# Second passes of a three-layer cross attention by blocks of four chunks, and a low-rank sum moved to a later layer

## The chip, the core and the metric

The kernel runs on one core of a Trainium2 chip. The metric is the device time of one execution in microseconds (us). A core has engines that run side by side, each with its own in-order queue: PE (TensorE: matrix products, the results in PSUM; PEld is its loading of the stationary operand), DVE (VectorE), ACT (ScalarE), POOL (GpSimd) and SP (SyncE, which here issues most of the transfers). An f32 matmul of the code leaves two records in the trace.

## The reference

A model of four layers works on x, 128 rows of 256. Every layer is a cross attention over a context of 12544 rows of 192, then a self attention over the 128 rows, then a mixture of eight experts (FFN); each is added to x after a layer norm. The change lies in the cross attentions of layers 0, 1 and 2, each of 16 heads of 16, and in two weights of layer 3's. In short, with scale 1/4:

```python
q, k, v = heads(x @ Wq + bq), heads(ctx @ Wk + bk), heads(ctx @ Wv + bv)
attn = einsum('bhqd,bhkd->bhqk', q, k) * scale   # 128 x 12544 scores for each of 16 heads
attn = clip(attn, -10000., 10000.)               # layer 1 only; layer 0 has a mask of keys
x = einsum('bhqk,bhkd->bqhd', softmax(attn), v) @ Wo + bo
```

In layer 3 the heads are 64 wide, and the key and value weights have a low-rank part: `k_in = ctx @ Wk + ctx @ k_down @ k_up * alpha / 32`, and the same for v.

## The kernel before

**Keys and groups.** The context's 12544 keys are 98 chunks of 128; four chunks make a block of `SB` = 512 keys (`NSB` = 25 blocks, the last of two chunks). The heads are worked on in two groups g of eight. Each head of 16 takes one of four row groups of 32 rows in the stationary operand, so `tiles` are four slices of 32 partitions and a "half" is two of them; s is which of two heads in a row group.

**PSUM in these layers.** `attend_twice` (L501) gives all of PSUM to four tiles from `self.pair()`, each 128 x 2 x 512 f32. While the second pass runs, one of them is `acc`, the weighted sums; so three rotate among the score groups. A new tile is the oldest one, and the instruction that first writes it waits until that one's last reader is through.

**First pass** (L607 to L614): for each block, `highest` makes the scores of two row groups (L538; in layer 0 with a mask added by a bf16 matmul, L537) and DVE takes their maximum over the keys (L539). Keys and values are projected between (`keys.project`, L102). The mask's rows come from `mask_rows` (L519): a transfer on SP's queue (L524), and two POOL operations (L526, L527), for each block.

**Between the passes** `lowered` (L541) turns minus the maximum into three bf16 parts, laid in `wide` and transposed (L556). `m` (L558) holds them as rows, copied twice side by side. In layer 1, `floor` (L633) is the lower limit of the clip.

**Second pass** (L638): a step of two chunks calls `weights` for half 0 and half 1 and then `weighted` for the step before (in layer 1 two steps before). `weights` takes a pair tile, adds minus the maximum with two bf16 matmuls of 512 (L567), and adds the products of keys and queries with four f32 matmuls of 256 (L575). The exponential goes to an SBUF tile `e` (4 of them, 6 in layer 1): in layer 0 by two ACT operations of 512, with the mask as a bias column for each chunk (L581); in layer 1 by a clip on DVE (helper L289, called at L586) and ACT in place (L587); in layer 2 by one ACT operation of 1024 (L583). `weighted` (L590) multiplies v, 17 columns with a one for the sum, by e: 16 f32 matmuls of 128 for two chunks (L595), added up in `acc`. After 49 steps DVE copies `acc` to `oT` (L649). The order on each engine is that of a scheduling framework; `in_order` (L224) makes the instructions of chosen engines stay as they were written.

**The low-rank part** of layer 3. `prepare_l3` (L959) runs in layer 0's cross attention as `between`: after block 3 of the first pass it loads alpha, the down and up factors and the two weights of 1 MB, and at the end of each group's first pass PE multiplies down by up (`mm`, L275, four f32 matmuls of 512 with 32 rows in each group) ahead of the transpose L556, and DVE adds the product times `rate` to the weight (L289). `keys_l3` (L1054) then projects early keys of layer 3 during layer 2's self attention and FFN: eight `early_pair` products (L102, tile `kv`, one pair of banks in turn), whose context comes by POOL's queue.

**FFN weights.** `large_weights` (L1676) has ten tiles of 1 MB in layers 0 and 2, four in the others. They are loaded by SP's queue as tiles come free.

Of the kernel before, what the change touches and what calls it, by code (L numbers as in the profile page):

```python
# [205 lines left out]
class Net:  # L206
    def __init__(self, tc, d, ctx):
# [9 lines left out]
        self.broad = pool("broad", 1)  # L217
        self.banks = ExitStack()
# [179 lines left out]
    def load_mask(self, pool):  # L398
# [20 lines left out]
        self.ts(mf, mf, 1.0, -NEG, ALU.subtract, ALU.mult)  # L419
        self.ts(mf, mf, self.any[:nr], None, ALU.mult)  # L420
        t = self.tr()
        nc.tensor.transpose(t[:, 0, :nr], mf, self.ident[:nr, :nr])
        self.mask_col = self.cp.tile([P, nr], F32, tag="maskcol", name="maskcol")
        nc.vector.tensor_copy(self.mask_col, t[:, 0, :nr])
# [82 lines left out]
    def attend_twice_in(self, pool, o, qz, keys, masked, clip, between):  # L507
# [5 lines left out]
        if masked:  # L513

            rows8 = [pool.tile([P, SB], U8, tag=f"mask{i}", name="mask", bufs=1) for i in range(3)]
            for r in rows8:
                nc.gpsimd.memset(r, 1)

        def mask_rows(g, b):  # L519

            src = d["mask"].rearrange("c p -> (c p)")[b * SB : min(S2, b * SB + SB)].unsqueeze(0)
            n = src.shape[-1]
            to = rows8[b % 3]
            nc.sync.dma_start(to[0:P:32, :n], src.to_broadcast([4, n]))  # L524
            row = pool.tile([P, SB], BF16, tag="row", name="row", bufs=3)
            nc.gpsimd.tensor_scalar(row[:, :n], to[:, :n], 0.0, 1.0, ALU.is_gt, ALU.subtract)  # L526
            nc.gpsimd.tensor_scalar(row[:, :n], row[:, :n], self.bar, None, ALU.mult)  # L527
            return row
# [32 lines left out]
        def weights(g, c, half, m, floor):  # L561


            x = self.pair()
            for i in range(2):
                r = tiles[2 * half + i]
                nc.tensor.matmul(x[:, i, :], self.ones16[r, :], m[r, :], start=True, stop=False, skip_group_check=True)  # L567
            kT = keys.kT(c // 4)
            for j in range(2):
                k = slice((c % 4 + j) * P, (c % 4 + j + 1) * P)  # L570
                for i in range(2):
# [3 lines left out]
                    nc.tensor.matmul(at, kT[r, k], q, start=False, stop=True, skip_group_check=True)  # L575
            e = pool.tile([P, 2, 2, 2, P], F32, tag="e", name="e", bufs=4 if clip is None else 6)
            to = e.rearrange("p i j s q -> p i (j s q)")
            if masked:
                for j in range(2):
                    part = slice(j * HB, (j + 1) * HB)  # L580
                    nc.scalar.activation(to[:, :, part], x[:, :, part], AF.Exp, bias=self.mask_col[:, c + j : c + j + 1])  # L581
            elif floor is None:
                nc.scalar.activation(to, x, AF.Exp)  # L583
            else:

                self.stt(to, x, 0.0, floor[half], ALU.min, ALU.max)  # L586
                nc.scalar.activation(to, to, AF.Exp)  # L587
            return e

        def weighted(g, c, es, acc):  # L590
            v = keys.v(c // 4)
            for j in range(2):
                for s in range(2):
                    for t in range(4):
                        nc.tensor.matmul(  # L595
                            acc[32 * t : 32 * t + 17, s, :P], v[:, c % 4 + j, 2 * t + s, :], es[t // 2][:, t % 2, j, s, :],
                            start=c + j == 0, stop=c + j == S2 // P - 1,
                        )

        for g in range(2):  # L600
# [6 lines left out]
            for b in range(NSB):  # L607
                if masked:
                    rows.append(mask_rows(g, b))
# [16 lines left out]
            if clip is not None:  # L626
                floor = []
                for half in range(2):
# [5 lines left out]
                    self.ts(floor[half], x, -clip, None, ALU.add)  # L634
            acc = self.pair()
            nc.vector.memset(acc[:, :, :P], 0.0)
            made = []
            for c in range(0, S2 // P, 2):  # L638
                made.append((g, c, [weights(g, c, half, m, floor) for half in range(2)], acc))
                if len(made) > (1 if clip is None else 2):  # L640
                    weighted(*made.pop(0))
# [4 lines left out]
            for step in made:  # L646
                weighted(*step)
# [213 lines left out]
    def l0_xattn(self, x):  # L861
        nc, d = self.nc, self.d
        with self.tc.tile_pool(name="x0", bufs=2, reuse_waits="tile") as pool:
# [15 lines left out]
            with self.tc.tile_pool(name="layer3", bufs=1, reuse_waits="tile") as other:  # L879
                self.attend_twice(o, qz, keys, masked=True, between=self.prepare_l3(other))  # L880
# [78 lines left out]
    def prepare_l3(self, pool):  # L959


        nc, d, own = self.nc, self.d, self.broad
        dims = H * 64
        self.rate = own.tile([P, 4], F32, tag="rate", name="rate")
        self.w3 = []
        parts = []

        def add_low(i, k, down, up, w):
            made = []

            def products(bank_pair):
                for c in range(2):
                    p = bank_pair()
                    for h in range(2):
                        self.mm(p[:, h, :], [(down[:, c * P : (c + 1) * P], up[:, h * 512 : (h + 1) * 512])])
                    made.append(p)

            def sums():
                for c, p in enumerate(made):
                    part = w[:, c, :].rearrange("p (h e) -> p h e", h=2)  # L980
                    self.stt(part, p, self.rate[:, i : i + 1], part, ALU.mult, ALU.add)

            return products, sums

        def load():
# [755 lines left out]
```

## Time and profile before

| what | us |
|---|---|
| median of three runs | 3110.43 (3102.11 to 3118.96) |
| profiled execution, its own time | 3103.82 |
| its span | 3102.1 |
| second passes of layer 0, both groups: windows 162.1 to 297, 438.9 to 568.6 | 134.9, 129.7 |
| of layer 1: 822 to 950.7, 1090.9 to 1214.9 | 128.7, 124.0 |
| of layer 2: 1502.7 to 1630, 1774 to 1894.7 | 127.3, 120.7 |
| layer 0's FFN weights, DMA share between 640 and 689 | 0.84 |
| layer 2's self attention, 1896 to 1950, DMA share | 0.94 |

The windows of the first groups hold some projections of the second group too, and those of layer 0 the low-rank products. The granted clock of PE was 0.973 of full speed over the span.

How the profile is read: a row of a group gives line, engine, operation, tiles written and read, shapes and how many, then busy us, mean ns of one, and the idle time of the engine before them with what ended it. A timeline row gives start, duration from first start to last end, engine, line, operation, tiles, and how many were put together; in brackets, how long the engine had been idle and what ended that. Many instructions of PE overlap, so starts tell more than ends.

### The profile page before, as it was taken

The page shows a single profiled execution, that of the slowest core. Times are in us where ns is not written, and L with a number is a line of the kernel's source. Part 1 is how long each engine was busy: PE and PEld are TensorE (multiplying, and loading weights), DVE is VectorE, ACT ScalarE, POOL GpSimd, SP SyncE. Part 2 cuts the span into 40 slices and gives each one's busy share as a digit, 9 for nine tenths or more (in the row PEclk, how much of TensorE's full clock was granted, in tenths as well). Part 3 has the DMA queues.
Part 4 walks back from the last instruction along what each step waited for, and adds up shares of the span by engine and source line. Part 5 has one row for each costly group of instructions (what it writes and reads, how often), then busy time and mean ns, then how long its engine had stood idle before and what let it go on. Part 6 is the DMA issues. An engine that isn't in the chain of part 4 may idle for free.

```text
span 3102.1 us, 78224 instructions
## 1 busy us (share of the span) xinstructions
PE 2958.3 (95%) x35065; PEld 2247.1 (72%) x35065; DVE 1954.4 (63%) x2300; ACT 1470.4 (47%) x1869; POOL 296.2 (10%) x349
## 2 busy tenths in 40 slices
PE   9999999879999999899999999899999999999979
PEld 6677667645576576665676576489889889889858
DVE  6811860439997897769208703467777777777854
ACT  1188139511383176311572275256556556556521
POOL 6600640112000000110000001000000000000000
PEclk9999999999999999999999999899999999999979
DMA  4100210552002102441102105332223232223436
GB/s 131 56 18 21 69 47 3 186 206 58 27 3 62 50 18 73 126 133 50 31 8 72 50 3 194 129 86 82 86 78 88 81 86 81 85 79 88 123 112 204
DMA packets 165254, 246.83 MB, mean 80 GB/s; under 512 B 19853, under 2 KB 106831, under 8 KB 164920
## 3 DMA queue, kind: packets, MB, share of 16 engines
q1 hardware_dynamic: 160200, 227.67, 24.1%
q0 software_dynamic: 4608, 14.16, 1.4%
q8 instruction: 275, 4.51, 0.6%
q14 instruction: 59, 0.48, 0.1%
q10 hardware_dynamic: 112, 0.01, 0.0%
HBM read 241.65 MB, written 0.13 MB: 78 GB/s over the span
## 4 chain that ended last, share of the span: by engine, by line
PE 80%; DVE 11%; ACT 5%; issue 2%; DMA 1%; POOL 1%; SPq 0%; DVEq 0%; ACTq 0%; POOLq 0%
PE pair L102 20%; PE pair L538 10%; PE pair L575 9%; PE pair L595 8%; PE v L102 7%; PE sc L701 6%; PE acc L743 5%; PE ps L275 4%; DVE parts L539 4%; ACT e L581 3%; PE pair L567 3%; PE kv L102 2%; PE acc L275 2%; PE ps L1532 1%; PE pair L537 1%
## 5 line engine op out<-in xcount | busy, mean ns | idle before, releaser
L539 DVE TENSOR_REDUCE parts<-pair 128x2 f32<-128x1024 f32 x600 | 679.1, 1197 | 103.7 <-PE pair L538 103.6
L102 PE MATMUL pair<-ctxA,wk 128*128 128x256 f32 x1236 | 328.9, 399 | 1.4 <-ACT kT L193 1.1
L649 DVE COPY oT<-pair 128x256 f32<-128x256 f32 x6 | 2.5, 424 | 508.4 <-PE pair L595 508.4
L102 PEld LDWEIGHTS pair<-ctxA,wk 128*128 128x128 f32 x1236 | 217.0, 190 | 140.0 <-DVE parts L539 96.0
L538 PE MATMUL pair<-kT,qz 32*128 32x512 f32 (+1 forms) x1632 | 277.7, 615 | 9.8 <-DVE parts L539 9.6
L703 ACT COPY kept<-sc 128x1024 f32<-128x1024 f32 (+1 forms) x135 | 136.3, 1009 | 261.3 <-PE sc L701 261.3
L286 DVE TENSOR_TENSOR top<-top,kept 128x1024 f32<-128x1024 f32 (+2 forms) x145 | 169.1, 1169 | 133.9 <-ACT kept L703 132.6
L575 PE MATMUL pair<-qz,kT 32*128 32x256 f32 x3168 | 251.6, 374 | 0.0
L581 ACT ACTIVATE e<-pair,maskcol 128x512 f32<-128x512 f32 x392 | 237.1, 688 | 18.7 <-PE pair L575 17.5
L289 DVE SCALAR_TENSOR_TENSOR e<-pair,floor 128x1024 f32<-128x1024 f32 x196 | 230.4, 1219 | 7.5 <-PE pair L575 1.7
L587 ACT ACTIVATE e<-e 128x1024 f32<-128x1024 f32 x196 | 207.2, 1057 | 38.5 <-DVE e L289 30.9
L583 ACT ACTIVATE e<-pair 128x1024 f32<-128x1024 f32 x196 | 189.9, 1021 | 60.2 <-PE pair L575 60.2
L595 PE MATMUL pair<-e,v 128*17 128x128 f32 x6336 | 212.3, 274 | 2.0 <-ACT e L587 1.0
L575 PEld LDWEIGHTS pair<-qz,kT 32*128 32x128 f32 x3168 | 205.3, 187 | 10.8
L132 ACT ACTIVATE kT<-pair,bk 128x512 f32<-128x512 f32 (+1 forms) x68 | 45.9, 674 | 346.8 <-PE pair L102 346.8
L595 PEld LDWEIGHTS pair<-e,v 128*17 128x17 f32 x6336 | 156.6, 97 | 67.1 <-issue 42.5
L701 PE MATMUL sc<-qz,kT 64*128 64x128 f32 x2816 | 197.8, 279 | 0.0
L567 PE MATMUL pair<-low,ones 32*128 32x512 bf16 x1176 | 191.7, 391 | 3.6 <-DVE low L558 3.1
L102 PEld LDWEIGHTS v<-wv,ctxA 128*128 128x128 f32 x1568 | 189.8, 192 | 6.4 <-issue 1.7
L102 PE MATMUL v<-wv,ctxA 128*128 128x128 f32 x1568 | 193.1, 276 | 0.0
L102 PE MATMUL pair<-ctxB,wk 64*128 64x256 f32 x1236 | 188.3, 398 | 0.0
L701 PEld LDWEIGHTS sc<-qz,kT 64*128 64x128 f32 x2816 | 171.6, 187 | 13.0 <-issue 1.3
(425 smaller groups left out, 4859.3 us busy)
## 6 DMA issues: line engine op xcount, KB each, us to landing
ctxA<-in_ctxA SPq DMA_DIRECT2D x324, 256.0 KB
ctxB<-in_ctxB SPq DMA_DIRECT2D x339, 128.0 KB
w<-in_L_ffn_W SPq DMA_DIRECT2D x32, 1024.0 KB
ctxA<-in_ctxA POOLq DMA_DIRECT2D x36, 256.0 KB, 3.6
w<-in_L_ffn_w_gateT SPq DMA_DIRECT2D x8, 1024.0 KB
wu<-in_L_ffn_w_upT SPq DMA_DIRECT2D x8, 1024.0 KB
w<-in_L_ffn_w_downT SPq DMA_DIRECT2D x8, 1024.0 KB
w<-in_L_ffn_w1T SPq DMA_DIRECT2D x8, 1024.0 KB
```

What stands on the lines that cost most here:

```text
L102: self.nc.tensor.matmul(out, a, b, start=start and not low, stop=low == 1, skip_group_check=True)
L275: self.nc.tensor.matmul(out, lhsT, rhs, start=(i == 0), stop=(i == n - 1))
L289: self.nc.vector.scalar_tensor_tensor(out, a, s, b, op0, op1, **kw)
L538: nc.tensor.matmul(x[:, i, :n], qz[r, g, s, :], keys.kT(b)[r, :n], start=not masked, stop=True)
L539: nc.vector.tensor_reduce(parts[:, s, 2 * half : 2 * half + 2, b], x[:, :, :n], AX.X, ALU.max)
L567: nc.tensor.matmul(x[:, i, :], self.ones16[r, :], m[r, :], start=True, stop=False, skip_group_check=True)
L575: nc.tensor.matmul(at, kT[r, k], q, start=False, stop=True, skip_group_check=True)
L581: nc.scalar.activation(to[:, :, part], x[:, :, part], AF.Exp, bias=self.mask_col[:, c + j : c + j + 1])
L583: nc.scalar.activation(to, x, AF.Exp)
L587: nc.scalar.activation(to, to, AF.Exp)
L595: nc.tensor.matmul(acc[32 * t : 32 * t + 17, s, :P], v[:, c % 4 + j, 2 * t + s, :], es[t // 2][:, t % 2, j, s, :], start=c + j == 0, stop= ...
L701: nc.tensor.matmul(x[:, t, c : c + P], kT[r, c : c + P], qz[r, g, :], start=True, stop=True)
```

## The change

1. The second pass goes by blocks of four chunks. `weights(g, b, ...)` makes four product groups (chunks 0 and 1 of half 0, then half 1, then chunks 2 and 3 of the same), then `weighted` of the block before is issued, 32 matmuls. There are eight e tiles (seven in layer 2), and DVE and ACT keep the written order.
2. Layer 0: the mask is added by the matmul that adds minus the maximum. Its stationary is a second set of mask rows made on POOL for each block of the second pass (a transfer, two POOL operations), with ones in rows 0 to 2 of each row group and the mask in row 3; it takes four matmuls of 256 for each group, with four loads of the stationary, instead of two of 512 with two. The exponential is then one ACT operation of 1024. The mask's column form and its transpose go.
3. Layer 2: minus the maximum of half 1 is spread once by PE and kept in `less`; DVE adds it to the scores while it copies them to e, and ACT takes the exponential in place, after both exponentials of half 0 of the block. Half 0 stays as it was.
4. The low-rank part leaves layer 0 and stands at the head of `keys_l3`: loads, DVE scaling of down by rate, on PE down times up plus the identity times the weight (16 f32 matmuls of 512), four ACT copies back. The weights lie in a pool of their own, the low-rank factors too, and the pool `narrow` is moved to the other side of the memory.
5. `large_weights` has 12 tiles in layer 0 and 9 in layer 2.

```diff
-        def mask_rows(g, b):
+        def mask_rows(b, second=False):
...
-            nc.gpsimd.tensor_scalar(row[:, :n], row[:, :n], self.bar, None, ALU.mult)
+            if second:
+                nc.gpsimd.tensor_scalar(row[:, :n], row[:, :n], self.bar, three, ALU.mult, ALU.add)
+            else:
+                nc.gpsimd.tensor_scalar(row[:, :n], row[:, :n], self.bar, None, ALU.mult)
...
+        def products(g, c, half, m, row):
+            x = self.pair()
+            kT = keys.kT(c // 4)
+            for i in range(2):
+                r = tiles[2 * half + i]
+                if row is not None:
+                    for j in range(2):
+                        at = slice(j * HB, (j + 1) * HB)
+                        k = slice((c % 4 + j) * P, (c % 4 + j + 1) * P)
+                        nc.tensor.matmul(x[:, i, at], row[r, k], m[r, at], start=j == 0, stop=False, skip_group_check=True)
+                elif m is not None:
+                    nc.tensor.matmul(x[:, i, :], self.ones16[r, :], m[r, :], start=True, stop=False, skip_group_check=True)
...
+        def weights(g, b, m, floor, less):
+            row = mask_rows(b, True) if masked else None
+            made, later = [], []
+            for c in range(4 * b, min(4 * b + 4, S2 // P), 2):
+                es = []
+                for half in range(2):
+                    by_dve = less is not None and half == 1
+                    x = products(g, c, half, None if by_dve else m, row)
+                    e = pool.tile([P, 2, 2, 2, P], F32, tag="e", name="e", bufs=7 if less is not None else 8)
...
+                    if by_dve:
+                        by_chunk = to.rearrange("p i (j n) -> p i j n", j=2)
+                        self.tt(by_chunk, x.rearrange("p i (j n) -> p i j n", j=2), bc(less, 2, 2), ALU.add)
+                        later.append(to)
+                    elif floor is not None:
+                        self.stt(to, x, 0.0, floor[half], ALU.min, ALU.max)
+                        nc.scalar.activation(to, to, AF.Exp)
+                    else:
+                        nc.scalar.activation(to, x, AF.Exp)
+                made.append((c, es))
+            for to in later:
+                nc.scalar.activation(to, to, AF.Exp)
+            return made
...
-            for c in range(0, S2 // P, 2):
-                made.append((g, c, [weights(g, c, half, m, floor) for half in range(2)], acc))
-                if len(made) > (1 if clip is None else 2):
-                    weighted(*made.pop(0))
+            last = []
+            with self.in_order(mybir.EngineType.DVE, mybir.EngineType.Activation):
+                for b in range(NSB):
+                    now = weights(g, b, m, floor, less)
+                    weighted(last, acc)
+                    last = now
...
+    def prepare_l3(self):
...
+        for i, k in ((1, "k"), (2, "v")):
+            w = self.load_kv(d[f"L3_xattn_W{k}"], dims, f"w{k}", self.wp3)
...
+            self.ts(down, down, self.rate[:RANK, i : i + 1], None, ALU.mult)
...
+            for c in range(2):
+                p = self.early_pair()
+                for h in range(2):
+                    cols = slice(h * 512, (h + 1) * 512)
+                    self.mm(p[:, h, :], [(down[:, c * P : (c + 1) * P], up[:, cols]), (self.ident, w[:, c, cols])])
+                nc.scalar.copy(w[:, c, :].rearrange("p (h e) -> p h e", h=2), p)
...
     def keys_l3(self):
+        self.prepare_l3()
...
-            with self.large_weights(bufs=10 if by_place else 4) as self.wp:
+            with self.large_weights(bufs={0: 12, 2: 9}.get(layer, 4)) as self.wp:
```

## The prediction, written before the result was known

> **What bounds the kernel now.** I read the page's engine lines, its chain of waits and its groups first, then the windows of the second passes one by one, then the timeline inside them.
>
> ```profile
> PE 2958.3 (95%) x35065; PEld 2247.1 (72%) x35065; DVE 1954.4 (63%) x2300; ACT 1470.4 (47%) x1869; POOL 296.2 (10%) x349
> ...
> PE 80%; DVE 11%; ACT 5%; issue 2%; DMA 1%; POOL 1%; SPq 0%; DVEq 0%; ACTq 0%; POOLq 0%
> ...
> L581 ACT ACTIVATE e<-pair,maskcol 128x512 f32<-128x512 f32 x392 | 237.1, 688 | 18.7 <-PE pair L575 17.5
> L289 DVE SCALAR_TENSOR_TENSOR e<-pair,floor 128x1024 f32<-128x1024 f32 x196 | 230.4, 1219 | 7.5 <-PE pair L575 1.7
> L587 ACT ACTIVATE e<-e 128x1024 f32<-128x1024 f32 x196 | 207.2, 1057 | 38.5 <-DVE e L289 30.9
> L583 ACT ACTIVATE e<-pair 128x1024 f32<-128x1024 f32 x196 | 189.9, 1021 | 60.2 <-PE pair L575 60.2
> ```
>
> TensorE is the bound (95% busy, 80% of the chain), so a PE that waits is lost time. The four groups read what a second pass writes to PSUM: ACT in layer 0 (L581), DVE then ACT in layer 1 (L289, L587), ACT in layer 2 (L583). The windows view (us; then busy PE, PEld, DVE, ACT, POOL; clock, DMA share, GB/s) gives one second pass of layers 0, 1 and 2:
>
> ```profile
> 162.10:297.00 134.90, 134.09 (x2607) 100.46 (x2606) 3.44 (x4) 122.27 (x202) 0.00 (x0) 0.96 0.05 15
> ...
> 1090.90:1214.90 124.00, 122.74 (x2552) 92.02 (x2546) 117.47 (x102) 103.61 (x98) 0.00 (x0) 1.00 0.03 7
> 1774.00:1894.70 120.70, 119.98 (x2548) 90.10 (x2548) 1.28 (x4) 96.06 (x99) 0.00 (x0) 1.00 0.01 3
> ```
>
> By the timeline, from the first L567 to the oT copy and without the 6.05 us of projections in each first group, the six passes last 124.0 and 124.8 (layer 0), 122 and 123.9 (layer 1), 121.4 and 120.5 us (layer 2): 49 steps of two chunks at 2.43 us. One steady step of layer 2:
>
> ```profile
> 1564.79 0.39 PE L567 MATMUL pair<-low,ones 32*128 32x512 bf16 x2
> 1565.01 0.38 PE L575 MATMUL pair<-qz,kT 32*128 32x256 f32 x2
> 1565.03 0.39 PE L567 MATMUL pair<-low,ones 32*128 32x512 bf16 x2
> 1565.23 1.05 PE L575 MATMUL pair<-qz,kT 32*128 32x256 f32 x14
> 1566.21 1.07 PE L595 MATMUL pair<-e,v 128*17 128x128 f32 x32
> 1567.21 0.39 PE L567 MATMUL pair<-low,ones 32*128 32x512 bf16 x2
> ```
>
> Two product groups (one per half; the halves use different rows of the array and overlap) take 1.42 us, the weighted sum 1.00. Two groups need two pairs of banks, three rotate (the fourth holds acc): a group finds its pair free.
>
> **Part 1: blocks of four chunks.** A block issues four groups, g1 to g4, and then the weighted sum of the block before (64 records instead of 32). With three rotating pairs, g4 takes the pair of g1 of its own block, and must wait until g1 has been computed and read. In the built order this holds in all three layers, and the weighted sum stands behind g4 on PE's in-order queue, so it can't fill the wait, and the next block's g1 and in the end the oT copy wait behind both. Before had this once: at the start of a pass no weighted sum stands between the first two steps. Layer 2, second group of heads:
>
> ```profile
> 1774.12 0.39 PE L567 MATMUL pair<-low,ones 32*128 32x512 bf16 x2 [0.79 <-DVE low L558]
> ...
> 1775.30 0.39 PE L567 MATMUL pair<-low,ones 32*128 32x512 bf16 x2
> ...
> 1775.48 3.77 ACT L583 ACTIVATE e<-pair 128x1024 f32<-128x1024 f32 x4 [6.11 <-PE pair L575]
> ...
> 1776.55 0.39 PE L567 MATMUL pair<-low,ones 32*128 32x512 bf16 x2
> ...
> 1777.73 1.07 PE L595 MATMUL pair<-e,kv 128*17 128x128 f32 x32
> ```
>
> g1 starts at 1774.12, its reader 1.36 later; spacing of readers is (3.77−1.02)/3 = 0.92; g4 starts at 1776.55, 2.43 after g1, though g1 and g2 needed 1.18 and g3 one half's work. From g4 to the weighted sum it is 1.18. So a block costs 1.36 + 1.07 (read, release) + 1.18 = 3.61, plus four chunks weighted at 1.89 (less one switch) to 2.00: **5.50 us where two steps took 4.85**.
>
> By layer. *Layer 0*: the mask enters by matmuls: per half 4 weight loads and 4 bf16 matmuls of 256 replace 2 and 2 of 512, the same columns; no row shows this form, so 0 (same columns) to +0.2 us per block (two extra 0.09 loads per half, half of them bare): 5.60. ACT does 4×0.92 = 3.7 instead of 8×0.61 = 4.88, hidden below PE now. POOL makes two rows per block (1.93 + 1.57 us by L526, L527), once more per pass, 25 mask DMAs more on SP's queue: 3.5 of 5.6 us, ahead of use, hidden; uncovered only if POOL were over 5.6. *Layer 1*: the reader is DVE at 1.22, so g4 starts at 1.36+1.22+0.05 = 2.63, block 5.70; DVE itself needs 4×1.13 = 4.52 (1.13 is the spacing in its unbroken runs), no longer the limit. *Layer 2*: half 1's subtraction goes from PE (L567) to DVE, g4 shortens from 1.18 to 0.96: 5.28 as lower bound. But DVE writes g4 into one of only seven e tiles, the one whose weighted sum of the block before is just running; ACT's exps are in order, so half 1's exps stand ahead of the next block's g1, and delay g4 there: weighted start +1.2 (tile free) +1.2 (DVE) + two exps of 1.13 puts the next g1's read 1.0 later: 5.6. I take 5.6, bounds 5.2 and 5.9.
>
> A pass has 24.5 blocks: the first without weighted sum 3.6, 23 at the period, 4.4 for the half block, its exps and two weighted sums. Layer 0: 3.6 + 23×5.6 + 4.4 = 136.8, plus 2 (10.2 us at half clock at the start of each pass): +14 each, **+28** (22 to 36). Layer 1: 3.8 + 23×5.7 + 4.9 + 1.5 (floors) = 141.3: **+36** (30 to 42). Layer 2: 136.8: **+31** (16 to 40).
>
> The Trainium skill, TensorEngine Tiling (Array Packing), section Key Properties, says that a change of tiling mode drains the array, which speaks for larger blocks, and its section PSUM Bottleneck warns that reading PSUM, not the array, may then bound and advises both ScalarE and VectorE as readers. The step above agrees with the first (1.42 for two groups before a switch, 1.18 in the run of four), by which alone the six passes would gain some 0.24×24.5×6 = 35 us; the second is what 1774 to 1777 shows, and by its advice layer 2 with two readers would be at its lower bound of 5.28, but g4 waits for one read, which a second reader doesn't shorten.
>
> **Part 2: layer 3's low-rank part.** It leaves layer 0's first passes, where its products stood on PE ahead of L556:
>
> ```profile
> 162.13 3.69 PE L275 MATMUL pair<-up,down 32*128 32x512 f32 x8
> 165.75 0.44 PE L556 MATMUL pair<-ident,wide 128*128 128x128 f32 x2
> ```
>
> That saves 2×3.65 = **−7.3**. It comes back ahead of the early keys of layer 3 in layer 2's attention and FFN: 12 DMAs on SP's queue, behind up to nine FFN weights of 1 MB (two weights of 1 MB in three DMAs each, two for each down, one for each up), 2 small DVE scalings, 16 f32 matmuls of 512, 4 ACT copies of 1024 (about 1.0 each). An f32 matmul leaves two records; eight of 32 rows take 3.69 here, eight of 128 rows take 3.70 in layer 2's attention (L275 at 1910.55), so 0.92 a matmul: 14.8 us. What waits for it are the eight early key pairs (2.9 to 3.0 us of PE each), which filled PE's gaps between 1896 and 1950, where DVE leads. Now one pair fits before the routing, one in the FFN's first gap, one is spread over the experts (PE-bound at 4.07 us each), and five stand between layer 3's norm and its query products: 5×2.9 = 14.5. PE's idle gaps (17 us in all at five places) take about the 14.8 of preparation if the weights are there at about 1928; DMA is full there (374 GB/s), and the 2 MB more take about 5.5 us. I take **+15**, bounds +5 (gaps take two pairs more) and +25 (weights late by 10).
>
> **Part 3: the rest.** Layer 0's FFN waits for weights: 13.98 and 15.51 us in its chain. Twelve buffers instead of ten let two loads of 1 MB start earlier; at 375 GB/s 2.8 us each, **−5** (0 to −10). The mask's transpose and the loads from 22 to 32 us go: −1 (0 to −2); the four alpha loads stay.
>
> Sum: 28 + 36 + 31 − 7.3 + 15 − 5 − 1 = **+97** on the profiled execution's own 3103.8 (span 3102.1): 3200.5. It lies 6.6 under the median of the runs shown, 3110.4, which spread by 17; half of that added: **3203**.
>
> **Rivals.**
> (a) *No stall*: the pairs free in time, for instance since reading begins before a group ends. Then four groups take 1.18+1.42−0.13 and the weighted sum 1.9: 4.4 per block (4.55 in layer 1, where DVE needs 4.52), a gain of 0.42×24.5×6 ≈ 60; with the +2 of the other parts about 3050 on the median's scale. For it: PE's work shrinks by switches, and layer 0's ACT limit (4.88) goes. Against it: 1774.12 to 1776.55. It decides if g4 starts less than 1.6 us after g1. 8%.
> (b) *Half a stall*: g4 waits in layers 0 and 1, but the DVE path in layer 2 and a weighted sum at 1.8 per block keep the period near 5.2: All six at 5.2 give 3.6 + 23×5.2 + 4.4 = 127.6 against a mean of 122.8: 6×4.8 + 2 = +31, or 3138. The records of 64 in a row aren't in the trace, which leaves room; the wait of 2.43 is. 10%.
> (c) *More than the stall*: weights of layer 3 late and the e-tile chain in layer 2 at 6.2 per block (+14 each), PE at half clock in some waits (the clock column falls to 0.88 between 1955 and 2010): 3245 to 3280. 12%.
> (d) *Nothing changes*, as only part 2 mattered: 2%.
> My forecast: 68%, own range 3170 to 3235.
>
> Under 0.5% (15 us) a measurement of this kernel can't tell from no change. Faster only in (a), 0.08; same in (d) and little of (b), 0.03; slower 0.89. The range leaves out (a), (d) and most of (c), and takes half of (b): 3148 to 3245.
>
> **What would show it.** In the profile after: second passes of 134 to 142 us; in each block a PE idle ahead of the fourth group, released by ACT (layers 0, 2) or DVE (layer 1), 2.4 to 2.65 us after g1's start; ACT in layer 0 busy 3.7 of 5.6; no L275 ahead of the transposes of layer 0; early-key products between layer 3's norm and queries; a shorter first FFN. Wrong if the fourth groups start without a wait, if a wait is filled by other PE work, or if layer 3's start waits for DMA.

## The result and the profile after

The changed kernel takes **3238.7 us** (median of 4 runs, 3236.8 to 3241.1) against 3111.9 for the kernel before; the ratio is 1.041, 95% interval 1.038 to 1.044. The profiled execution took 3236.75, its span is 3235.1, 133.0 longer than before's; the medians differ by 126.8.

These rows of the page answer to those shown of before; the first is the engines' busy time, the second the share of the chain of waits by engine, the others are groups.

```profile
PE 3058.0 (95%) x35280; PEld 2342.0 (72%) x35280; DVE 2071.2 (64%) x2396; ACT 1422.3 (44%) x1677; POOL 429.4 (13%) x453
...
PE 74%; DVE 15%; ACT 7%; issue 2%; DMA 1%; POOL 1%; SPq 0%; DVEq 0%; ACTq 0%; POOLq 0%
...
L619 ACT ACTIVATE e<-pair 128x1024 f32<-128x1024 f32 x294 | 280.8, 1026 | 99.8 <-PE pair L594 99.6
...
L291 DVE SCALAR_TENSOR_TENSOR e<-pair,floor 128x1024 f32<-128x1024 f32 x196 | 226.3, 1217 | 50.5 <-ACT e L617 49.1
...
L617 ACT ACTIVATE e<-e 128x1024 f32<-128x1024 f32 x196 | 207.2, 1057 | 77.3 <-DVE e L291 66.5
...
L288 DVE TENSOR_TENSOR e<-pair,less 128x1024 f32<-128x1024 f32 x98 | 120.0, 1225 | 145.8 <-PE pair L631 97.3
```

PE is still busy 95% of the span, which alone would hide what happened: its share of the chain fell from 80 to 74%, and DVE and ACT took over these 6 points, because PE now waits for them. The readers of PSUM have more idle time (layer 1's clip, L291, has 50.5 us ahead of it instead of 7.5), and so has layer 1's exponential behind it (L617, 77.3 instead of 38.5).

Where the 133 us are, by marks that both traces have (the first maximum, the copy to `low` at the end of a first pass, the copy to `oT` at the end of a second, the end):

| stage | before | after | difference |
|---|---|---|---|
| start to the first `low` | 166.2 | 172.6 | +6.4 |
| second passes of layer 0 (`low` to `oT`) | 130.8, 125.5 | 141.6, 136.2 | +21.5 |
| second passes of layer 1 | 129.0, 124.9 | 148.6, 144.1 | +38.8 |
| second passes of layer 2 | 128.2, 121.3 | 143.1, 136.6 | +30.2 |
| layer 0, first pass of the second group | 143.9 | 140.2 | −3.7 |
| `oT` of layer 0 to layer 1's first maximum (attention, FFN) | 124.3 | 120.6 | −3.7 |
| last `oT` of layer 2 to the end | 1207.4 | 1245.9 | +38.5 |
| all others (the largest: first pass of layer 2's first group, +3.5) | | | +5.0 |

A block of layer 0 in the timeline (start and duration, engine, line, operation). The rows of L585 at 226.64, 227.74 and 229.08 open g1, g3 and g4, the first, third and fourth product group; the one at 232.15 opens the next block:

```profile
226.64 0.39 PE L585 MATMUL pair<-low,row 32*128 32x256 bf16 x4
...
227.74 0.27 PE L585 MATMUL pair<-low,row 32*128 32x256 bf16 x2
...
227.96 1.03 PE L594 MATMUL pair<-qz,kT 32*128 32x256 f32 x8
...
228.01 3.77 ACT L619 ACTIVATE e<-pair 128x1024 f32<-128x1024 f32 x4 [1.73 <-PE pair L594]
...
229.08 0.40 PE L585 MATMUL pair<-low,row 32*128 32x256 bf16 x4
...
229.30 1.04 PE L594 MATMUL pair<-qz,kT 32*128 32x256 f32 x8
...
230.28 1.94 PE L631 MATMUL pair<-e,v 128*17 128x128 f32 x64
...
232.15 0.39 PE L585 MATMUL pair<-low,row 32*128 32x256 bf16 x4
```

g1 starts at 226.64, ACT reads it from 228.01 (1.37 later) to about 229.03, and g4 starts at 229.08, 2.44 after g1; 1.20 later the weighted sum, and 5.51 after g1 the next block. PE is hardly idle ahead of g4: the last record of g3 ends at 228.99, 0.09 before it. What is lost is overlap, for g3 now runs alone and g4 alone. Layer 1 shows the same with DVE as reader:

```profile
906.48 0.39 PE L587 MATMUL pair<-low,ones 32*128 32x512 bf16 x2
...
907.86 4.62 DVE L291 SCALAR_TENSOR_TENSOR e<-pair,floor 128x1024 f32<-128x1024 f32 x4 [1.09 <-ACT e L617]
...
909.11 3.32 ACT L617 ACTIVATE e<-e 128x1024 f32<-128x1024 f32 x3 [1.26 <-DVE e L291]
909.13 0.39 PE L587 MATMUL pair<-low,ones 32*128 32x512 bf16 x2 [0.32 <-DVE e L291]
...
909.35 1.04 PE L594 MATMUL pair<-qz,kT 32*128 32x256 f32 x8
...
910.32 1.94 PE L631 MATMUL pair<-e,v 128*17 128x128 f32 x64
...
912.19 0.39 PE L587 MATMUL pair<-low,ones 32*128 32x512 bf16 x2
```

The fourth group names its releaser itself (DVE's write of e, which read the pair). The block takes 5.71; it is longer than layer 0's by the reader's 1.22 instead of 1.02. In layer 2, where DVE reads half 1:

```profile
1642.62 1.23 DVE L288 TENSOR_TENSOR e<-pair,less 128x1024 f32<-128x1024 f32 x1 [2.09 <-PE pair L631]
...
1643.34 0.39 PE L587 MATMUL pair<-low,ones 32*128 32x512 bf16 x2
...
1644.85 1.96 ACT L619 ACTIVATE e<-pair 128x1024 f32<-128x1024 f32 x2
...
1645.90 1.13 PE L594 MATMUL pair<-qz,kT 32*128 32x256 f32 x8 [0.24 <-ACT e L619]
...
1648.84 0.39 PE L587 MATMUL pair<-low,ones 32*128 32x512 bf16 x2
```

g1 starts at 1643.34 and g4, which ACT's read of g1 releases, 2.56 later; the block takes 5.50. DVE's write of half 1 waits for an e tile that the weighted sum is still reading, and its exponential puts off the read of g1, to 1.51 behind g1's start.

The second large part lies behind layer 2. The windows view (us; busy PE, PEld, DVE, ACT, POOL; clock, DMA share, GB/s) of its self attention and the routing behind it, after the change and then, in the last row, of the attention before:

```profile
1998.00:2030.00 32.00, 20.70 (x61) 13.76 (x61) 19.22 (x37) 5.71 (x9) 0.00 (x0) 0.61 0.87 301
2030.00:2052.00 22.00, 20.81 (x45) 9.24 (x44) 3.41 (x11) 5.65 (x7) 0.00 (x0) 0.58 0.16 35
2052.00:2074.00 22.00, 21.22 (x39) 8.79 (x38) 9.22 (x40) 2.23 (x3) 1.08 (x3) 0.50 0.05 13
...
1904.00:1930.00 26.00, 22.29 (x113) 14.72 (x112) 19.97 (x38) 8.17 (x11) 8.04 (x15) 1.00 1.06 375
```

The third number from the end is the granted clock: 0.61, 0.58, 0.50. Before, 26 us of the same attention (1904 to 1930) ran at 1.00 with PE busy 22.3. From oT to the routing's `place` product it takes 85.4 us instead of 58.8 (+26.6); the FFN's experts up to layer 3's norm are as before (+0.7), and the queries of layer 3, with early key pairs among them, make the remaining 11.2. The low-rank products can't fill the attention's gaps, since all but one of their sixteen matmuls come late: the first starts at 1990.82, the second, which is the first to use the key weight, at 2030.33, 41.2 us after oT.

### The profile page after: what moved, and what is told of

It reads as the page before. It is cut to its first block, busy times and chain, and to the rows that moved or that the text cites. A ratio compares the mean times of both kernels' runs of the same rounds, so it can differ in the third digit from the quotient of the medians.

```text
span 3235.1 us, 78791 instructions
## 1 busy us (share of the span) xinstructions
PE 3058.0 (95%) x35280; PEld 2342.0 (72%) x35280; DVE 2071.2 (64%) x2396; ACT 1422.3 (44%) x1677; POOL 429.4 (13%) x453
## 4 chain that ended last, share of the span: by engine, by line
PE 74%; DVE 15%; ACT 7%; issue 2%; DMA 1%; POOL 1%; SPq 0%; DVEq 0%; ACTq 0%; POOLq 0%
PE pair L102 19%; PE pair L543 9%; PE v L102 7%; PE pair L594 7%; PE pair L631 6%; PE sc L741 6%; PE acc L783 5%; PE ps L277 4%; DVE parts L544 4%; ACT e L619 3%; DVE e L291 3%; PE kv L102 2%; DVE e L288 2%; PE acc L277 2%; PE ps L1556 1%
## 5 line engine op out<-in xcount | busy, mean ns | idle before, releaser
L102 PE MATMUL pair<-ctxA,wk 128*128 128x256 f32 x1236 | 329.9, 400 | 1.4 <-ACT kT L193 1.1
L619 ACT ACTIVATE e<-pair 128x1024 f32<-128x1024 f32 x294 | 280.8, 1026 | 99.8 <-PE pair L594 99.6
L594 PE MATMUL pair<-qz,kT 32*128 32x256 f32 x3168 | 312.6, 379 | 7.6 <-ACT e L619 7.6
L102 PEld LDWEIGHTS pair<-ctxA,wk 128*128 128x128 f32 x1236 | 217.7, 191 | 140.6 <-DVE parts L544 96.7
L543 PE MATMUL pair<-kT,qz 32*128 32x512 f32 (+1 forms) x1632 | 276.3, 610 | 10.3 <-DVE parts L544 10.1
L594 PEld LDWEIGHTS pair<-qz,kT 32*128 32x128 f32 x3168 | 240.8, 186 | 37.1 <-ACT e L619 20.5
L291 DVE SCALAR_TENSOR_TENSOR e<-pair,floor 128x1024 f32<-128x1024 f32 x196 | 226.3, 1217 | 50.5 <-ACT e L617 49.1
L617 ACT ACTIVATE e<-e 128x1024 f32<-128x1024 f32 x196 | 207.2, 1057 | 77.3 <-DVE e L291 66.5
L528 POOL TENSOR_SCALAR row<-mask 128x512 bf16<-128x512 uint8 (+1 forms) x100 | 189.2, 1892 | 234.3 <-PE pair L585 120.9
L288 DVE TENSOR_TENSOR e<-pair,less 128x1024 f32<-128x1024 f32 x98 | 120.0, 1225 | 145.8 <-PE pair L631 97.3
L631 PE MATMUL pair<-e,v 128*17 128x128 f32 x6336 | 193.4, 273 | 1.5 <-ACT e L617 1.1
L102 PEld LDWEIGHTS v<-wv,ctxA 128*128 128x128 f32 x1568 | 189.9, 192 | 6.4 <-issue 1.7
L102 PE MATMUL v<-wv,ctxA 128*128 128x128 f32 x1568 | 193.1, 276 | 0.0
L631 PEld LDWEIGHTS pair<-e,v 128*17 128x17 f32 x6336 | 164.6, 98 | 34.6 <-issue 21.2
L102 PE MATMUL pair<-ctxB,wk 64*128 64x256 f32 x1236 | 188.4, 398 | 0.0
```

The source lines that it names most:

```text
L102: self.nc.tensor.matmul(out, a, b, start=start and not low, stop=low == 1, skip_group_check=True)
L288: self.nc.vector.tensor_tensor(out, a, b, op)
L291: self.nc.vector.scalar_tensor_tensor(out, a, s, b, op0, op1, **kw)
L543: nc.tensor.matmul(x[:, i, :n], qz[r, g, s, :], keys.kT(b)[r, :n], start=not masked, stop=True)
L594: nc.tensor.matmul(at, kT[r, k], q, start=m is None and j == 0, stop=True, skip_group_check=True)
L631: nc.tensor.matmul(acc[32 * t : 32 * t + 17, s, :P], v[:, c % 4 + j, 2 * t + s, :], es[t // 2][:, t % 2, j, s, :], start=c + j == 0, stop= ...
```

## The experiments

All ratios are against the kernel before, from runs on the same chip.

**Steps of two chunks in the changed kernel.**

```diff
-                for b in range(NSB):
-                    now = weights(g, b, m, floor, less)
-                    weighted(last, acc)
-                    last = now
+                for c in range(0, S2 // P, 2):
+                    last.append(weights(g, c, m, floor, less))
+                    if len(last) > (1 if clip is None else 2):
+                        weighted(last.pop(0), acc)
```

> The changed kernel with the second passes back in steps of two chunks (weighted sum one step behind, two in layer 1); mask by matmul, subtraction on DVE in layer 2, the low-rank part in layer 2 and all buffers stay as changed. Theory (g4 waits for the reader of g1): the six passes fall from 141.6, 136.2, 148.6, 144.1, 143.1, 136.6 us (from the copy to low to the copy to oT) to about 131, 125.5, 129, 125, 128, 121, some 90 us in all; 3237 becomes about 3147, still slower than before by 35 to 40. Rival (the longer weighted sums, the mask matmuls or the kept order of ACT and DVE make the passes longer): layers 0 and 2 stay above 135, and the time stays above 3190. If DVE's subtraction in layer 2 helps once PSUM is free, its passes fall to 112 to 118.

3141.6 us, ratio 1.010 (1.008 to 1.011). The six passes take 127.0, 122.0, 129.0, 124.2, 127.7 and 122.0: 98 us less, the whole loss and a little more. So the block length is what costs; with the mask matmuls, the kept order and the e tiles in place the passes are as short as before. Layer 2 gained nothing from DVE's subtraction, where 112 to 118 had been thought possible. Its timeline shows this:

```profile
1560.87 1.22 DVE L288 TENSOR_TENSOR e<-pair,less 128x1024 f32<-128x1024 f32 x1 [1.30 <-PE pair L594]
...
1562.13 1.06 ACT L624 ACTIVATE e<-e 128x1024 f32<-128x1024 f32 x1 [0.35 <-DVE e L288]
...
1563.00 1.29 PE L633 MATMUL pair<-e,v 128*17 128x128 f32 x32
```

DVE and then ACT are through with half 1 at 1563.19, for a weighted sum that starts at 1563.00 and takes 1.29 instead of 1.07; steps alternate between 2.30 and 2.53. So one step of lag looks too short for two engines in a row; a longer one was not tried.

**The weighted sum between g3 and g4.**

```diff
                 for half in range(2):
                     by_dve = less is not None and half == 1
+                    if half == 1 and (c % 4 == 2 or c + 2 == S2 // P):
+                        weighted(last, acc)
```

> The changed kernel with the weighted sum of the block before issued between the third and the fourth group, so that PE works while g1 is read. Theory: no wait of PE in layers 0 and 2, but g3 and g4 no longer overlap on the array: g1 and g2 1.18, g3 1.18, weighted 1.9, g4 1.1, so 5.3 to 5.4 per block against 5.51 measured, 5.3 in layer 1 against 5.71; the time falls by 6 x 24 x 0.15 to 0.4, so 20 to 50 us, to 3190 to 3215, not to the 4.85 of two steps. Rival (the wait for the pair isn't what costs): no change. Rival (a free PE does the four groups in 2.6 and the sum in 1.9 wherever it stands): 4.5 per block, 3100.

3253.9, ratio 1.046 (1.044 to 1.047): a miss. Blocks take 5.51 in layer 0 and 5.71 in layer 1, to the hundredth what they took before the move (5.57 instead of 5.50 in layer 2). In layer 0:

```profile
224.68 0.39 PE L585 MATMUL pair<-low,row 32*128 32x256 bf16 x4
...
227.12 0.40 PE L585 MATMUL pair<-low,row 32*128 32x256 bf16 x4
...
230.19 0.39 PE L585 MATMUL pair<-low,row 32*128 32x256 bf16 x4
```

The fourth group of the run again starts 2.44 after the first. I had overlooked that between two weighted sums there are still four groups in a row, now g4, g1, g2, g3, and the fourth of any such run over three pairs waits for the first one's reader. What counts is the length of the run between sums, not where in the block the sum stands. It is 15 us slower than the changed kernel; in the profiles most of that lies in the second passes of layer 1 (+1.2, +3.0) and of layer 2 (+2.0, +4.4) and between layers 0 and 1 (+4.9); why was not followed.

**Four rotating pairs.**

```diff
-            acc = self.pair()
-            nc.vector.memset(acc[:, :, :P], 0.0)
...
-                    weighted(last, acc)
+                    if last:
+                        weighted(last, self.pair())
```

> The changed kernel with four rotating pairs instead of three: the weighted sum of a block goes to a pair of its own that comes from the same ring and is added to nothing. It leaves out adding the blocks up (the output is the last block's alone); every product, read, exponential and weighted sum of the changed kernel is still there. Theory (blocks of four are slow only because the fourth group waits for the first one's pair): no wait of PE ahead of g4, 4.4 to 4.5 us per block in layer 0 instead of 5.51, about 4.55 in layer 1 (DVE needs 4.52) instead of 5.71, 4.4 to 4.7 in layer 2; passes of some 112 to 121 us, 24 to 28 less each, and about 3085 in all, below the kernel before. Rival (long runs of 64 weighted records or of four groups are slow by themselves, or the readers set the pace): blocks stay above 4.85 and the time above 3130.

3087.8, ratio 0.993 (0.992 to 0.995), for a kernel that leaves out adding the blocks' sums up. Layer 0:

```profile
225.03 0.40 PE L585 MATMUL pair<-low,row 32*128 32x256 bf16 x4
...
226.13 0.28 PE L585 MATMUL pair<-low,row 32*128 32x256 bf16 x2
...
226.37 0.38 PE L585 MATMUL pair<-low,row 32*128 32x256 bf16 x4
226.56 1.06 PE L594 MATMUL pair<-qz,kT 32*128 32x256 f32 x14
227.55 1.94 PE L631 MATMUL pair<-e,v 128*17 128x128 f32 x64
229.43 0.39 PE L585 MATMUL pair<-low,row 32*128 32x256 bf16 x4
```

g3 (226.13) and g4 (226.37) overlap again, as g1 and g2 do; g4 starts 1.34 after g1 instead of 2.44, and the block takes 4.40. One pair of banks makes the difference between 5.51 and 4.40; blocks of four are 0.46 better than two steps of 2.43 when the pairs are there. Layer 1 gains less (passes of 124.6 and 120.2, blocks of 4.62 to 4.67), for DVE's four clips alone had been reckoned at 4.52 a block.

**The alphas later.**

```diff
-        self.rate = self.broad.tile([P, 4], F32, tag="rate", name="rate")
+        self.rate = self.wp3.tile([P, 4], F32, tag="rate", name="rate")
...
-            alpha = self.all_rows(d[f"L3_xattn_{name}_alpha"], 1, f"a{name}", self.sp)
+            alpha = self.wp3.tile([P, 1], F32, tag=f"a{name}", name=f"a{name}")
+            nc.sync.dma_start(alpha, d[f"L3_xattn_{name}_alpha"].to_broadcast([P, 1]))
```

> The changed kernel, with the four alphas and their rates in a pool that opens in layer 2, so that neither loads nor DVE operations can stand in layer 0. Theory: the first first-pass of layer 0 was longer by 11 us (152.7 against 141.3 from its first maximum to low) because DVE waited 8.2 us for the first alpha ahead of a maximum, and PE then ran at half clock; it falls to 141 to 143 (less the 3.7 of the low-rank products: 138 to 140), the time by 10 to 14 to about 3225. Rival (the second mask rows and memsets on POOL hold up the first pass): no change in that stage.

3233.3, ratio 1.039 (1.037 to 1.041). The stage from the first maximum to `low` falls from 152.7 to 142.3; since its first maximum is 2.3 later, the first `low` comes 8.1 earlier (164.5 instead of 172.6). Behind layer 2 4.3 us are given back, so that the whole gains 5 instead of the 10 to 14 expected, and the interval of its ratio overlaps the changed kernel's. What it took away stands in the changed kernel's timeline:

```profile
30.43 0.15 DVE L295 TENSOR_SCALAR rate<-aq 128x1 f32<-128x1 f32 x1 [8.16 <-DMA aq<-in_L_xattn_q_alpha]
...
33.64 0.62 PE L542 MATMUL pair<-row,ones 32*128 32x512 bf16 x2 [7.54 <-DVE parts L544]
34.02 1.94 PE L543 MATMUL pair<-kv,qz 32*128 32x512 f32 x4
```

DVE waits 8.16 us for a transfer of 512 bytes that stands behind others on SP's queue, the maxima behind it wait, PE waits 7.54 for those, and then runs at half speed: the same four L543 records took 1.02 to 1.04 us before the wait, and the granted clock is 0.50 from 33.6 to 37.

**The low-rank part ahead of the self attention.**

```diff
     def keys_l3(self):
-        self.prepare_l3()
...
             if layer == 2:
...
+                self.prepare_l3()
```

> The changed kernel with the low-rank part called ahead of layer 2's self attention, so that its weights are loaded ahead of the FFN's and the early keys of layer 3 may again fill PE's gaps in the attention. Theory (in the changed kernel the part from oT of layer 2 to the end is 38.6 us longer, since the early keys no longer fill the attention, PE falls to half clock there from 1992 to 2074, and 16 matmuls take 2.0 us instead of 0.92): the tail falls by 15 to 30 us, the clock in the attention is above 0.9, the early keys end before layer 3's queries; 3237 becomes 3207 to 3222. Rival (the transfers bound that stage, 2 MB more): the tail stays within 5 us of the changed kernel's.

3213.9, ratio 1.033 (1.031 to 1.035). The part behind layer 2's last `oT` falls from 1245.9 to 1222.2, by 23.7: its weights come first, the early keys lie in the attention again, and from 2024 the clock is 1.00.

```profile
2005.48 2.08 PE L277 MATMUL kv<-wk,ident 128*128 128x512 f32 x2
...
2012.19 1.12 PE L277 MATMUL kv<-up,down 32*128 32x512 f32 x2
```

The preparation itself ran at 2.0 us a matmul, from start to start, up to 2009 and at 1.05 from 2010.

**A hundred matmuls more.**

```diff
     def keys_l3(self):
+        p = self.early_pair()
+        for i in range(100):
+            self.mm(p[:, i % 2, :P], [(self.ident, self.ident)])
         self.prepare_l3()
```

> The changed kernel with 100 f32 matmuls of 128x128 more on PE (identity by identity, used by nothing, 0.2 us each at full clock, some 22 us of added work) at the head of the low-rank part; they lie in PE's gaps of layer 2's self attention, ahead of the low-rank products. Theory (PE fell to half clock in that stage because the early keys no longer filled its gaps): the granted clock there rises from 0.5 to 0.6 to above 0.9, the low-rank matmuls take 0.95 to 1.15 us instead of 2.0, the part from layer 2's last oT to the end falls by 8 to 18 us although PE has more to do, and the time from 3238 to some 3222 to 3230. Rival (the weights' late arrival or the order of work alone makes that stage longer): no gain, or 5 to 20 us longer by the added work.

3226.6, ratio 1.035 (1.031 to 1.040). With 25.0 us of useless PE records added, the part behind layer 2 is 11.8 us *shorter* (1234.1). The same window as above:

```profile
1998.00:2030.00 32.00, 31.84 (x239) 28.25 (x237) 20.16 (x39) 6.30 (x10) 0.00 (x0) 1.00 0.92 311
```

DMA is as busy as it was, and the key weight's first product starts as late (40.3 us after oT instead of 41.2). So the low clock had cost that part of the time, and not the transfers; what the weights' late arrival costs besides was not tested alone. Ten of the sixteen low-rank matmuls took the 0.95 to 1.15 us expected; five, between 2040 and 2051, took 1.9 to 2.1.

**A version that beats both.** Layers 0 and 2 in blocks of four with four rotating pairs, the sum of a block added by DVE to a total in SBUF; layer 1 in steps of two; the low-rank part ahead of the attention; the alphas late.

```diff
+        def summed(made, total):
+            x = self.pair()
+            weighted(made, x, (made[0][0], made[-1][0] + 1))
+            for t in range(4):
+                r = slice(32 * t, 32 * t + 17)
+                self.tt(total[r], total[r], x[r, :, :P], ALU.add)
```

> A version meant to be faster than both: blocks of four chunks in layers 0 and 2 with four rotating pairs, the weighted sum of a block read by DVE and added to a total in SBUF (four operations of 17 rows); layer 1 in steps of two chunks; layer 2 without the subtraction on DVE; the low-rank part ahead of layer 2's self attention, the alphas late. Theory: 4.4 to 4.5 us per block in layers 0 and 2, passes of 111 to 118 there, 129 and 124 in layer 1; from 3138.6 (the run of two-chunk steps) 40 less for these four passes, 24 for the low-rank part's place, 4 to 8 for the alphas: 3065 to 3075, 1.2 to 1.5% below the kernel before. Rival (the added reads on DVE delay the pairs, or e tiles run out): over 4.85 per block and no gain over 3111.

3129.7, ratio 1.006 (1.004 to 1.009): a miss, and its rival named the cause.

```profile
225.24 0.39 PE L585 MATMUL pair<-low,row 32*128 32x256 bf16 x4
...
225.38 1.76 DVE L288 TENSOR_TENSOR total<-total,pair 17x256 f32<-17x256 f32 x4 [3.26 <-PE pair L634]
...
227.20 0.28 PE L585 MATMUL pair<-low,row 32*128 32x256 bf16 x2
```

With five tiles per block over four pairs, g4 takes the pair of the sum before. Four additions of 17 rows take 1.76 us, end at 227.14, and g4 starts at 227.20: 5.02 us per block. The same with layer 2's subtraction on DVE:

> As the run without the subtraction on DVE, but layer 2 keeps it (half 1), with eight e tiles. Theory: PE saves the L587 matmuls of half 1, 0.1 to 0.25 us per block, if DVE (two subtractions of 1.22 and four adds of about 0.4, 4.0 us per block) and ACT (two of 0.92 and two of 1.13, 4.1) keep up: layer 2's passes 0 to 6 us shorter than without it. Rival: the pairs of half 1 are held longer and the fourth exponential comes too late for the weighted sum, layer 2's passes 3 to 10 us longer.

3123.5, ratio 1.005 (1.003 to 1.007); layer 2's passes 132.6 and 125.8 against 132.8 and 126.2, hardly a difference while the additions hold up g4. So the four additions became one of 128 rows, for which the weighted sum takes 32 columns of v (the 15 more belong to other heads; their sums are not used):

```diff
-                                acc[32 * t : 32 * t + 17, s, :P], v[:, c % 4 + j, 2 * t + s, :], ...
+                                acc[32 * t : 32 * t + n, s, :P], v[:, first : first + n], ...
...
-            for t in range(4):
-                r = slice(32 * t, 32 * t + 17)
-                self.tt(total[r], total[r], x[r, :, :P], ALU.add)
+            self.tt(total, total, x[:, :, :P], ALU.add)
```

> As the run with four rotating pairs and a total in SBUF, but one DVE addition of 128 rows and 256 columns instead of four of 17 rows (the weighted sum takes 32 columns of v instead of 17, so that all rows are written; the 15 more hold other heads' sums that nothing uses). In that run a block took 5.02 us, since the fourth group took the pair of the sum, and that was free only when the four additions (1.76 us) were through. Theory: one addition of about 0.45 ends well before the fourth group is due; 4.39 us per block as in the ring without additions, four passes shorter by 24 x 0.63 = 15 each; 3125 becomes 3065, ratio to before 0.985. Rival: loading 32 columns instead of 17 makes the weighted sums longer, 4.39 is missed by over 0.2 and the ratio stays above 0.992.

> As the run before it, with half 1's subtraction on DVE in layer 2 and eight e tiles. With the four additions gone DVE needs 2 x 1.25 + 0.45 = 2.95 and ACT 4.3 us per block. Theory: PE's block in layer 2 is 0.1 to 0.2 shorter than without it (4.2 to 4.3), 3 to 10 us in all against the run without; or ACT's 4.3 us become the limit and nothing is gained (within 3 us). Rival: the later exponentials delay the weighted sums, and layer 2's passes are longer.

3063.5, ratio **0.984** (0.981 to 0.986) without and 3061.2, ratio **0.983** (0.980 to 0.985) with the subtraction on DVE. Layer 0's passes are 116.8 and 111.2 in both, layer 2's 117.6 and 110.5 without and 117.0 and 109.6 with it. A block of layer 0, with the one addition in 0.42:

```profile
223.57 0.40 PE L585 MATMUL pair<-low,row 32*128 32x256 bf16 x4
...
223.70 0.42 DVE L288 TENSOR_TENSOR total<-total,pair 128x256 f32<-128x256 f32 x1 [3.98 <-PE pair L636]
...
224.91 0.38 PE L585 MATMUL pair<-low,row 32*128 32x256 bf16 x4
```

g4 is again 1.34 behind g1; 32 columns instead of 17 made nothing longer (64 records of the sum in 1.95, against 1.94). Between the two versions the intervals overlap: the subtraction on DVE gains 1.5 us in layer 2's passes (blocks of 4.33 instead of 4.39), within the 3 us that were to count as nothing gained.

## Why the prediction was right, and where a size was off

**Part 1, the stall: right, in mechanism and size.** The blocks take 5.51, 5.71 and 5.50 us where 5.60, 5.70 and 5.60 were forecast; the six passes lost 90.5 where the sum had 95 (layer 0 21.5, just under its range, layer 1 38.8, layer 2 30.2). Two-chunk steps gave all of it back, the fourth pair too, and moving the sum inside the block nothing, which together leave only the run of four groups over three pairs. One sign was read too simply: a PE idle ahead of g4 was forecast for each block, but it is 0.09 us in layer 0, 0.32 in layer 1 and 0.24 in layer 2. The 1.10 us by which g4 comes later than with four pairs are mostly the lost overlap of g3 and g4. In layer 2 the chain over e tiles and ACT's order came as described, but it put off the read of g1 by 0.15 us, where 1.0 had been reckoned.

**Layer 0's clock, a term that did not come.** The sum added 2 us to each pass for the half-speed start. After the change the clock is 1.00 from 172.6 on, where before it was 0.50 for 10.2 us: layer 0 lost 10.8 and 10.7 instead of 14 (the block of 5.51 instead of 5.60 makes another 2.1 of it). That start had come behind the low-rank products, which are gone; the two-chunk run has neither and its passes are 3.8 and 3.5 below before's. The link between the two is seen in the traces, not tested alone. Nor is the half clock gone: a shorter stretch of it now lies ahead of `low` (granted 0.50 from 167 to 169), where the value projections L102 take 3.18 and 1.61 us instead of 2.05 and 1.16.

**Part 2, the low-rank part: the mis-sized term.** The forecast had −7.3 + 15 = +8 with an upper bound of +25 on the second. Measured are −3.7 in the second group of layer 0, +6.4 up to the first `low`, and +38.5 behind layer 2. Two steps of the prediction failed:
- "PE's idle gaps … take about the 14.8 of preparation" took 0.92 us a matmul from rows at full clock, and weights that are there at about 1928, 33 us after oT. The product that needs the first of them started 41.2 after oT, close to the attention's end (its output product stands at 2037.36), and thirteen of the sixteen matmuls took 1.9 to 2.1 us, for PE had fallen to half clock once the early keys no longer filled the attention's gaps; the attention's own products, which are on the path, ran at half clock too. Together this is +26.6 up to the routing, where I had put nothing. Of that the added matmuls gave back 14.7, which shows the clock's part, and the earlier preparation 9.9, which agrees with the missing fill. The rest isn't separated: the preparation's own work, the late weights, and the half clock that those two runs still have. Half clock was named in rival (c), with the right column of the right view, but was kept out of the sum.
- "the four alpha loads stay" had no price. They stay in the kernel but moved on the queues: DVE's rate operations now stand ahead of maxima and behind a late transfer. Their cost is 8.1 us up to the first `low`, by the run without them. With the 1.6 us of half clock ahead of `low` and the 3.7 of products saved this makes 6.0 of the 6.4.

The early pairs at layer 3's queries cost 11.2 where 14.5 was worked out: four of the five stand between the query products, at 2.95 to 2.99 us each, and the fifth runs while the norm is worked out.

**Part 3.** The stage with layer 0's FFN gained 3.7 where 5 was taken; the larger pool of buffers was not tested alone. POOL's second mask rows are hidden, as forecast: POOL is busy about half of the time in layer 0's pass (66.0 us in the 135.3 from 179 on), and with four pairs the block falls to 4.40 under the same work of POOL. The −1 for what leaves the start can't be told apart: the first maximum comes 5.0 us earlier (19.9 instead of 24.9), and the wait for the alphas follows it.

**Rivals.** (a) was excluded by the 2.44 us between g1 and g4; its price of 60 us against before was right, the four-pair run's passes are together 58 below before's. (b) and (d) fell with it. Of (c) the clock came true, and the weights were late, by some 8 us if the product that first needs them is the measure; with the clock kept up, the same late weights cost 11.8 less in spite of 25 us of work added. Its block of 6.2 in layer 2 did not come. The time, 3238.7, lies 36 above the forecast, inside the range of 3148 to 3245, but 4 above the main case's own, 3170 to 3235: it is the stall as forecast, with the clock of rival (c) and the wait for the alphas added.

## What to carry to other kernels

Before lengthening a run of products, count the buffers that it rotates through: with n buffers, the group n+1 of a run waits for the first one to be computed *and* read, and work behind it on the same in-order queue doesn't fill that wait; moving that work to another place in the loop changes nothing while the run stays as long. The loss may show as missing overlap of two groups and not as idle time. If the buffer that is missing holds an accumulator, adding each block's sum to SBUF on an idle engine can free it, in one wide operation rather than several narrow ones, since that read holds a buffer too. When work is moved out of gaps of TensorE, price the stage that is left at half clock as well, and look up where the moved step's smallest loads and scalings come to stand on every queue.

## What the runs showed of the hardware

- PE could be busy 96% of a stretch and stay at half clock: it was busy 21.2 of 22 us between 2052 and 2074, with a granted clock of 0.50, in a stretch of mostly f32 matmuls of 512 columns, alternately on 128 and on 32 rows. In the run with the low-rank part first, the same chain stayed at 2.0 us a matmul until 2009 and then went at 1.05; in the run with a hundred more it fell back to 2.0 between 2040 and 2051. The Trainium skill (TensorE: Matmul & The Clock Gate, section What's actually happening) has the clock return after some 3.4 us of sustained work; these 22 us did not bring it back. What sets this chain apart was not tested.
- Loading 32 stationary columns instead of 17 left the weighted sum as long as it was (1.95 against 1.94 us for 64 records).
- Four DVE additions of 17 rows and 256 columns take 1.76 us, 0.44 each, and one of 128 rows 0.42: here the number of operations cost time, the number of rows did not.
